# A four-layer attention kernel on Trainium2: the output projection of an item in halves between the next item's scores, and a plainer end of the quantised layer's stages

## The chip, the cores and the metric

The kernel runs on one core of one Trainium2 chip. The metric is the device time of one execution in microseconds (us). Before the change three runs gave 2229.62, 2235.7 and 2238.51 us; the median is 2235.7 us. All times in this text are measured on the chip; "at 1092.91" means so many us after the start of the profiled execution.

The core has five engines that run side by side, each through its own list of instructions in a fixed order: TensorE (PE, matrix products into the accumulator memory PSUM), VectorE (DVE), ScalarE (ACT), GpSimd (POOL), and SyncE (SP), which here issues transfers (DMA). An instruction waits on semaphores for the results that it needs, and everything behind it in its engine's list waits with it.

## The reference

Four layers work on x of 8 items x 256 tokens x 320 channels, with a context of 120 tokens x 192 channels for each item.

- L0: self attention, cross attention over the context, and a gated feed-forward part, each added to x. Its attention is quantised in the reference's way: q, k and v are each divided by (largest absolute value of the whole tensor / 127), rounded to whole numbers and multiplied back; the softmax weights are rounded likewise, in steps of (largest weight / 255). There are 20 heads of 16 channels.
- L1: self attention, cross attention and a gated feed-forward part, not quantised.
- L2: attention over the first 104 context tokens and, with a softmax of its own, over the last 16; both are summed and projected. In the profile this is "both".
- L3: attention with 8 heads over the context and over a few further tokens whose queries are made through x itself. In the profile this is "last".

In short, for one attention with residual:

```python
q, k, v = fq_sym(x @ Wq), fq_sym(ctx @ Wk), fq_sym(ctx @ Wv)      # fq_sym only in L0
w = softmax(einsum('bhnd,bhmd->bhnm', q, k) * dh ** -0.5)
w = fq_zero(w)                                                    # only in L0
x = x + einsum('bhnm,bhmd->bhnd', w, v).reshape(b, n, c) @ Wo + bo
```

## The kernel before

**Two parts.** `tile_xattn_kernel` (L1622) first runs L0's two attentions through two objects of class `Quant`, `s` for self and `c` for cross. Since a quantisation step needs the largest value of the whole tensor, these go stage by stage over all eight items. All other work is `run_flow` (L667): 40 items (four feed-forward blocks of L0, then eight self, eight cross, four feed-forward, eight "both", eight "last") in a pipeline.

**The order of the work.** The kernel is written as generators. `weave` (L649) and `run_flow` take one step of each live generator in turn, and what a step issues is put at the end of the engines' lists. A scheduler behind it may still move single instructions within an engine. So the order in which generators are taken in a round, and the places of their `yield`s, set which of two pieces of work comes first on each engine.

**`run_flow`.** At step s it runs four generators: `tops` of item s+1 (largest scores), `project` of item s+2 (norm, transposes, q, k, v), `fin` of item s-1 (output projection), and `out` of item s (softmax and values), in this order before the change. Within one item of heads:

- `top_scores` (L398): `max_scores` (L374) makes the scores of a query tile against all keys on PE (L385) into PSUM pairs, and DVE takes the negated largest value of each row (L392, `negm`). PE then transposes `negm` (L409), ScalarE copies it to `nT`, and five transfers on SP put it into rows of `qT` (`qT<-nT`), so that the next pass subtracts the maximum within the product.
- `weighted` (L415): `exps(g)` makes the scores again, transposed (L430), and ScalarE the exponentials (`e`, L436); `values` multiplies them with v and with ones (L447); DVE's reciprocal (L455) and multiply (L456) give `oT`. There are five head groups; `exps(0)` comes before the first `yield`, then one group for each round.
- `project_out_steps` (L472): the residual with bias on POOL (L477); then for each of the two token tiles t a `yield`, the product of `oT` with the output weights (L120: three matmuls of 128x320, five for "both", where `oT` has five parts), and the addition to x on DVE (L483). `out` ends with the first step of it, so `fin` has the two halves left. The reductions, the scores and the transposes work on PSUM tiles in rotation: `pair()` (`pf`) and `bank()` (`pa`).

**The quantised layer.** `project_all` (L1207) makes q, k and v of each self item; ScalarE copies them from PSUM (`Q`, `K`, `V`), and `top` (L1201) takes the largest absolute values on DVE (L1202). The last item's q and k are read in PSUM directly, in four reductions. `steps` (L1319) brings the maxima of all partitions together through two transposes (L489 to L496) and makes the steps (`sc`). `whole` (L1339) turns q and k of an item into whole numbers in bf16, in five passes: `tk` and `tq` (scaled, with a large constant added, L1347 and L1350), the constant subtracted from `tk` twice under two masks of heads (`K`, L1353 and L1357), and from `tq` (`Q`, L1363 or L1362). For item 0 (`fast`) DVE takes `tk` and `K`, POOL `tq`, and ScalarE `Q`; all other items go through `whole_all` (L1390) on POOL, except item 1 of the cross part, which is `fast` too. `tops_all` (L1407) makes the scores (L1422) and their maxima (L1425). `out_all` (L1547) makes weights, values (L1563) and the output projection; alongside it, `queries_all` (L1284) makes the cross part's q: `norm`, `turn` (transposes, L330), three `project`s for each item, at rounds of a table `at`.

Of the kernel before, what the change touches and what calls it, by code (L numbers as in the profile page):

```python
# [18 lines left out]
P = 128  # L19
# [35 lines left out]
class Kernel:  # L55
# [118 lines left out]
    def open_quant(self, pool):  # L174

        nc = self.nc

        self.place = pool.tile([P, G, PAD], F32, name="place")
        nc.gpsimd.memset(self.place, 0.0)
        for g in range(G):  # L180
            nc.gpsimd.memset(self.place[:, g, 15 + g : 30 : G], 1.0)

        self.magic = pool.tile([P, 1], F32, name="magic")
        nc.gpsimd.memset(self.magic, -MAGIC)
        self.fill = pool.tile([P, 1], F32, name="fill")
        self.rows = pool.tile([P, 3], F32, name="rows")
        for i in range(3):
            nc.vector.tensor_reduce(self.rows[:, i : i + 1], self.m32[:, 15 + G * i : 30], AX.X, ALU.add)
        nc.vector.tensor_scalar(self.fill, self.rows[:, 0:1], -1e6, 1e6, ALU.mult, ALU.add)
        nc.vector.tensor_scalar(self.rows[:, 1:], self.rows[:, 1:], -1.0, None, ALU.mult)  # L190
        self.sel = pool.tile([P, 2, G, P], BF16, name="sel")
        col = pool.tile([P, 2, G], F32, name="selc")
        for i in range(2):
            nc.vector.tensor_reduce(
                col[:, i], self.m32[:, : 15 * (i + 1)].rearrange("p (i g) -> p g i", g=G), AX.X, ALU.add
            )
            nc.vector.tensor_copy(self.sel[:, i], col[:, i].unsqueeze(2).to_broadcast([P, G, P]))
        self.npx = pool.tile([P, TPB, 4, PAD], BF16, name="npx")
        nc.gpsimd.memset(self.npx, 0.0)
        self.nTs = pool.tile([P, B, N], BF16, name="nTs")  # L200
        self.sums = pool.tile([P, B, N], F32, name="sums")
# [196 lines left out]
    def top_scores(self, qT, kT, nk, segs):  # L398

        nc = self.nc  # L400
        negm = self.small.tile([P, len(segs), 4, G, TPB], F32, tag="negm", name="negm")
        yield from self.max_scores(qT, kT, nk, segs, negm)
        yield
        nT = self.work.tile([4 * G, len(segs), N], F32, tag="nT", name="nT", bufs=1)
        for n in range(len(segs)):
            ps = self.bank()
            nv = negm[:, n].rearrange("p j g t -> p (j g) t")
            for t in range(TPB):
                nc.tensor.transpose(ps[: 4 * G, t * P : (t + 1) * P], nv[:, :, t], self.ident)  # L409
            nc.scalar.copy(nT[:, n, :], ps[: 4 * G, :N])  # L410
            for g in range(G):
                r = n if g in (1, 3) else D + n
                nc.sync.dma_start(qT[r::PAD, g, :], nT[g::G, n, :])
# [253 lines left out]
    def run_flow(self, items, before={}, after={}):  # L667


        n = len(items)  # L670
        made = {}
        for step in range(-2, n + 1):
            if step + 2 < n:
                if step + 2 in before:
                    before[step + 2]()
                made[step + 2] = items[step + 2]()
            order = ((step + 1, 1), (step + 2, 0), (step - 1, 3), (step, 2))
            gens = [made[i][k]() for i, k in order if 0 <= i < n]
            while gens:
                for g in list(gens):  # L680
                    try:
                        next(g)
                    except StopIteration:
                        gens.remove(g)
            if step in after:
                after[step]()

# [492 lines left out]
class Quant:  # L1180
# [5 lines left out]
    def __init__(self, k, pool, kpool, ln, w, brow, cross):  # L1186
        self.k, self.pool, self.kpool, self.ln, self.w, self.brow, self.cross = k, pool, kpool, ln, w, brow, cross
        self.kc, self.ks = (1, M) if cross else (TPB, P)
        self.nk = self.kc * self.ks

        per = 2 // self.kc
        self.units = [(range(g, min(G, g + per)), h) for g in range(0, G, per) for h in range(2)]
        nc = k.nc
        n = "c" if cross else "s"
        self.am = pool.tile([P, 3, B + 2], F32, name=f"am_{n}")
        nc.gpsimd.memset(self.am, 0.0)
        self.sc = pool.tile([P, 16], F32, name=f"sc_{n}")
        self.q, self.kk, self.v = {}, {}, {}


    def top(self, i, b, src):  # L1201
        self.k.nc.vector.tensor_reduce(  # L1202
            self.am[: src.shape[0], i, b : b + 1], src, AX.XY if len(src.shape) > 2 else AX.X, ALU.max,
            apply_absolute_value=True,
        )

    def project_all(self):  # L1207
# [11 lines left out]
        for b in range(B):  # L1219
# [26 lines left out]
                nc.scalar.copy(dst[:, :2], ps[:, :, :N])  # L1246
                nc.scalar.copy(dst[:, 2], ps[:, i, N:])
            self.top(2, b, v)
            if b + 1 < B:
                self.top(0, b, q)  # L1250
                self.top(1, b, kt)
                continue

            for i, ps in enumerate((pq, pk)):
                self.top(i, b, ps[:, :, :N])
            for i, ps in enumerate((pq, pk)):
                self.top(i, B, ps[:, i, N:])

    def keys_all(self):

# [23 lines left out]
    def queries_all(self):  # L1284
# [4 lines left out]
        def norm(b):  # L1289
            x[b] = k.normed(b, self.ln, on=nc.gpsimd if b + 1 < B else None)  # L1290
# [6 lines left out]
        def project(b, m):  # L1297
            ps = k.pair()
            k.mm(ps[:, 0, :N], [(w["q"][:, c, m * P : (m + 1) * P], xT[b][:, c, :]) for c in range(3)])
            nc.scalar.copy(self.q[b][:, m * N : (m + 1) * N], ps[:, 0, :N])  # L1300
            if b + 1 == B:
                self.top(0, b + m, ps[:, 0, :N])
            elif m == 2:
                self.top(0, b, self.q[b])

        at = {b: [5 * b + i for i in (0, 3, 6, 7, 8)] for b in range(B - 2)}
        at[B - 2] = [5 * B - 10 + i for i in (0, 3, 4, 5, 7)]
        at[B - 1] = [5 * B - 10 + i for i in (3, 6, 7, 8, 9)]  # L1310
        for r in range(5 * B):
            for b in range(B):
                for i, n in enumerate(at[b]):
                    if n == r:
                        norm(b) if i == 0 else turn(b) if i == 1 else project(b, i - 2)
            yield


# [20 lines left out]
    def whole(self, b, fast=False):  # L1339
# [4 lines left out]
        to = nc.vector if fast else nc.gpsimd  # L1344
        q, kt = self.q[b], self.kk[b]
        tk = k.work.tile([P, 3 * N], F32, tag="xT", name="tk")
        to.tensor_scalar(tk[:, : 3 * nk], kt, sc[:, 7:8], MAGIC, ALU.mult, ALU.add)  # L1347
        yield
        tq = k.work.tile([P, 3 * N], F32, tag="xh", name="tq")
        nc.gpsimd.tensor_scalar(tq, q, sc[:, 6:7], MAGIC, ALU.mult, ALU.add)  # L1350
        yield
        kh = self.kk[b] = kt.bitcast(BF16)[:, : 5 * nk].rearrange("p (c n) -> p c n", n=nk)
        to.tensor_scalar(  # L1353
# [5 lines left out]
        )  # L1359
        yield  # L1360
        qh = self.q[b] = q.bitcast(BF16)[:, : 3 * N].rearrange("p (c n) -> p c n", n=N)
        if fast:  # L1362
            nc.scalar.activation(qh.rearrange("p c n -> p (c n)"), tq, AF.Identity, bias=k.magic)  # L1363
        else:
            to.tensor_scalar(qh.rearrange("p c n -> p (c n)"), tq, MAGIC, None, ALU.subtract)

    def whole_v(self, b):

# [21 lines left out]
    def whole_all(self):  # L1390

        for b in range(1, B):
            n = 0
            for _ in self.whole(b, self.cross and b == 1):
                n += 1
                yield
            for _ in range(len(self.units) - n):
                yield
# [115 lines left out]
    def weight_steps(self):  # L1514
# [3 lines left out]
        nc.scalar.activation(k.sums, k.sums, AF.Ln)  # L1518
        part = k.small.tile([P, 2], F32, tag="part", name="part")
        least = k.small.tile([P, 1], F32, tag="least", name="least")  # L1520
        nc.vector.tensor_reduce(least, self.am[:, 0, :B], AX.X, ALU.min)
        nc.vector.reciprocal(part[:, 0:1], least)
        most = k.small.tile([P, 2], F32, tag="most", name="most")
        if self.cross:
            nc.vector.tensor_reduce(part[:, 1:2], self.am[:, 2, :B], AX.X, ALU.max)
            k.all_max(most, part)
            nc.vector.tensor_copy(sc[:, 2:3], most[:, 1:2])
            self.step_of(2, 3)
        else:
            k.all_max(most[:, :1], part[:, :1])  # L1530
# [16 lines left out]
    def out_all(self):  # L1547
# [42 lines left out]
            pass  # L1590
        self.shift(0)
        todo, projects = [], {}
        for r in range(rounds * B + 2):
            b, i = divmod(r, rounds)
            if b < B:
                w = weights(b, groups[i])
                if i == 0:
                    more = self.whole_v(b + 1) if b + 1 < B else iter(())
                todo.append((b, groups[i], w))
            while len(todo) > (2 if b < B else 0):  # L1600
                values(*todo.pop(0))


            for t in range(TPB):
                d, left = divmod(r - 2 - t, rounds)
                if r == rounds * B + 1:
                    d, left = B, 0
                if left == 0 and 1 <= d <= B:
                    if t == 0:
                        projects[d] = project(d - 1)  # L1610
# [11 lines left out]
def kernel(ctx: ExitStack, tc: tile.TileContext, a, out):  # L1622
    k = Kernel(ctx, tc, a, out)
    with ExitStack() as es:
# [15 lines left out]
        with tc.tile_pool(name="l0", bufs=1) as pool:  # L1640
            k.open_quant(pool)
            with tc.tile_pool(name="l0_keys", bufs=1, side="right") as kpool:
# [10 lines left out]
                    c.top(1, b, c.kk[b])  # L1653
                s.weight_steps()
                v = c.values_all()
                k.weave((0, s.out_all()), (8, c.queries_all()), (5 * B + 1, islice(v, 3)))
            fp = ff.enter_context(tc.tile_pool(name="w_ff1", bufs=1, side="right"))
            context = ExitStack()
            k.open_context(context.enter_context(tc.tile_pool(name="context", bufs=1, side="right")), dram)
# [133 lines left out]
```

## Time and profile before

| What | Before |
|---|---|
| median of three runs | 2235.7 us |
| profiled execution | 2235.43 us |
| its span (first to last instruction) | 2233.4 us |
| mean granted TensorE clock, share of full speed | 0.965 |
| L0's two attentions, 0 to about | 672 us |
| self items of L1, a step | 38.1 us |
| cross items of L1, a step | 22.5 us |
| "both" items, a step | 25.3 us |

The profile is one execution on the chip. Its group rows read: line, engine, operation, output<-inputs, shape and type, x count | busy us, mean ns of one | idle us of the engine just before them, and what ended most of it. The tables of waits give: who waits at which line, "<-" the engine and line that released it: us in all, times, longest. The timelines give: start in us, duration in us, engine, line, operation, x count, and in brackets the idle time before. A matmul of 32*128 uses 32 rows of the array, four of them running side by side; one of 128*128 uses it whole.

### The profile page before, as it was taken

The page shows a single profiled execution, that of the slowest core. Times are in us where ns is not written, and L with a number is a line of the kernel's source. Part 1 is how long each engine was busy: PE and PEld are TensorE (multiplying, and loading weights), DVE is VectorE, ACT ScalarE, POOL GpSimd, SP SyncE. Part 2 cuts the span into 40 slices and gives each one's busy share as a digit, 9 for nine tenths or more (in the row PEclk, how much of TensorE's full clock was granted, in tenths as well). Part 3 has the DMA queues.
Part 4 walks back from the last instruction along what each step waited for, and adds up shares of the span by engine and source line. Part 5 has one row for each costly group of instructions (what it writes and reads, how often), then busy time and mean ns, then how long its engine had stood idle before and what let it go on. Part 6 is the DMA issues. An engine that isn't in the chain of part 4 may idle for free.

```text
span 2233.4 us, 38265 instructions
## 1 busy us (share of the span) xinstructions
PE 2044.5 (92%) x16413; PEld 1201.3 (54%) x16413; DVE 1117.4 (50%) x1698; ACT 825.7 (37%) x1252; POOL 357.9 (16%) x365
## 2 busy tenths in 40 slices
PE   6889878898899999999999999899999799999997
PEld 5643345554444555465555555554555455666664
DVE  4388677555752221335655667611121466556465
ACT  2347878467532121124444443411201233222221
POOL 1092066601411000000000001100000100000100
PEclk9989889898889999999999999999999899999999
DMA  4000000642110000020000001100000201000000
GB/s 117 17 12 2 1 1 4 167 111 57 55 53 28 1 0 1 1 92 2 2 2 22 27 25 35 47 1 0 1 1 2 68 25 32 12 24 26 23 19 16
DMA packets 79303, 63.21 MB, mean 28 GB/s; under 512 B 48410, under 2 KB 68318, under 8 KB 78622
## 3 DMA queue, kind: packets, MB, share of 16 engines
q1 hardware_dynamic: 75070, 57.06, 9.3%
q10 hardware_dynamic: 4064, 3.71, 0.6%
q8 instruction: 129, 2.11, 0.4%
q14 instruction: 40, 0.33, 0.1%
HBM read 42.61 MB, written 17.37 MB: 27 GB/s over the span
## 4 chain that ended last, share of the span: by engine, by line
PE 75%; DVE 16%; ACT 5%; issue 3%; DMA 1%; POOL 1%; SPq 0%; ACTq 0%; DVEq 0%; POOLq 0%
PE pf L120 13%; PE pf L584 13%; PE pf L132 9%; PE pa L120 7%; PE pa L447 6%; PE pf L430 4%; PE pa L584 3%; PE pf L139 3%; PE pf L385 3%; DVE negm L1425 3%; PE pf L1466 3%; PE pf L728 3%; DVE rs L455 2%; PE pa L1488 2%; DVE negm L392 2%
## 5 line engine op out<-in xcount | busy, mean ns | idle before, releaser
L436 ACT ACTIVATE e<-pf 128x1024 f32<-128x1024 f32 (+2 forms) x176 | 158.3, 944 | 234.9 <-PE pf L430 227.8
L392 DVE TENSOR_REDUCE negm<-pf 128x4 f32<-128x1024 f32 (+4 forms) x224 | 188.1, 886 | 108.8 <-PE pf L385 108.8
L584 PE MATMUL pf<-xTf,ff 128*128 128x512 f32 x512 | 232.4, 601 | 5.2 <-DVE negm L392 5.2
L455 DVE RECIPROCAL rs<-pa 128x256 f32<-128x256 f32 x88 | 152.2, 1745 | 144.0 <-PE pa L447 144.0
L477 POOL TENSOR_TENSOR xb<-x_sb,brow 128x640 f32<-128x640 f32 x40 | 62.2, 1555 | 792.2 <-DVE x_sb L483 748.2
L1473 ACT ACTIVATE e<-pf,sc_s 128x1024 f32<-128x1024 f32 x160 | 169.6, 1116 | 49.4 <-PE pf L1466 42.6
L1425 DVE TENSOR_REDUCE negm<-pf 128x4 f32<-128x1024 f32 (+2 forms) x128 | 143.3, 1134 | 68.1 <-PE pf L1422 61.4
L611 DVE SCALAR_TENSOR_TENSOR hT<-pf,cols_sb,gl 128x512 f32<-128x512 f32 x64 | 48.0, 751 | 256.8 <-ACT gl L610 254.5
L120 PE MATMUL pf<-ff,hT 128*128 128x320 f32 x640 | 174.4, 434 | 0.0
L584 PEld LDWEIGHTS pf<-xTf,ff 128*128 128x128 f32 x512 | 94.9, 191 | 125.2 <-issue 119.8
L120 PEld LDWEIGHTS pf<-ff,hT 128*128 128x128 f32 x640 | 120.9, 190 | 55.5 <-issue 6.1
L430 PE MATMUL pf<-qT,kT 32*128 32x256 f32 (+1 forms) x1280 | 122.3, 411 | 21.9 <-DMA qT<-nT 12.8
L610 ACT ACTIVATE gl<-pf,cols_sb 128x512 f32<-128x512 f32 x64 | 43.9, 687 | 248.0 <-PE pf L584 248.0
L385 PE MATMUL pf<-kT,qT 32*128 32x120 f32 (+1 forms) x1920 | 114.8, 329 | 18.3 <-ACT e L436 18.1
L120 PE MATMUL pa<-o,oT 128*128 128x320 f32 x352 | 105.4, 441 | 15.2 <-DVE oT L456 14.1
L385 PEld LDWEIGHTS pf<-kT,qT 32*128 32x128 f32 x1920 | 84.9, 189 | 58.4 <-ACT e L436 27.7
L1466 PE MATMUL pf<-Q,K 32*128 32x256 bf16 (+1 forms) x960 | 90.5, 294 | 25.3 <-DVE negm L1425 13.2
L639 POOL TENSOR_TENSOR xb<-x_sb,brow 128x640 f32<-128x640 f32 x16 | 25.1, 1566 | 543.1 <-DVE x_sb L644 528.7
L447 PE MATMUL pa<-e,v 128*32 128x256 f32 (+1 forms) x1280 | 105.2, 388 | 2.3 <-ACT e L436 1.7
L1581 DVE TENSOR_SCALAR w<-e 128x1024 bf16<-128x1024 f32 (+2 forms) x128 | 87.4, 691 | 37.5 <-ACT e L1473 36.3
L430 PEld LDWEIGHTS pf<-qT,kT 32*128 32x128 f32 (+1 forms) x1280 | 68.7, 183 | 68.3 <-issue 37.3
L132 PE MATMUL pf<-xT,q 128*128 128x256 f32 x384 | 101.0, 392 | 0.4 <-ACT e L436 0.2
(287 smaller groups left out, 3448.1 us busy)
## 6 DMA issues: line engine op xcount, KB each, us to landing
ff<-in_L_xattn_Wff_dram SPq DMA_DIRECT2D x1, 2560.0 KB
qT<-nT SPq DMA_DIRECT2D x160, 4.0 KB
ff<-in_L_xattn_ff_w_dram SPq DMA_DIRECT2D x1, 2560.0 KB
out_dram<-x_sb SPq DMA_DIRECT2D x16, 160.0 KB
kd_cross<-kst SPq DMA_DIRECT2D x8, 300.0 KB
vd_cross<-vst SPq DMA_DIRECT2D x8, 300.0 KB
vd_both<-vst SPq DMA_DIRECT2D x8, 300.0 KB
kT<-kd_cross SPq DMA_DIRECT2D x8, 300.0 KB
```

The lines of the kernel that those rows point to most:

```text
L120: self.nc.tensor.matmul(out, l, r, start=i == 0, stop=i == len(pairs) - 1)
L132: self.nc.tensor.matmul(o, *t[c], start=start and c == 0, stop=stop and c == n - 1, skip_group_check=True)
L385: nc.tensor.matmul(s[j // 2][:, j % 2, o : o + nk], qT[r : r + PAD, g, t * P : (t + 1) * P], kT[r : r + PAD, g, :nk], start=True, stop=True,)
L392: nc.vector.tensor_reduce(negm[:, n, 2 * i : 2 * i + 2, g0 : g0 + len(gs), :].rearrange("p j g t -> p j (g t)"), sv[:, :, :, k0:k1], AX.X, ...
L430: nc.tensor.matmul(s[j // 2][:ks, j % 2, o : o + N], kT[r : r + PAD, g, c * ks : (c + 1) * ks], qT[r : r + PAD, g, :], start=True, stop=True,)
L436: nc.scalar.activation(e[:ks, 2 * i : 2 * i + 2, :n], s[i][:ks, :, :n], AF.Exp, scale=scale)
L447: nc.tensor.matmul(o[j * PAD : (j + 1) * PAD, what * N : (what + 1) * N], w, es[g][:ks, j, c * N : (c + 1) * N], start=first and c == 0 an ...
L455: nc.vector.reciprocal(rs, o[:, N:])
L584: ins = nc.tensor.matmul(*args, **kw)
L1425: nc.vector.tensor_reduce(negm[:, 2 * h : 2 * h + 2, gs[0] : gs[-1] + 1, :].rearrange("p j g t -> p j (g t)"), s[:, :, : len(gs) * TPB * n ...
L1466: nc.tensor.matmul(s[at // 2][:ks, at % 2, o : o + N], l, m, start=not shift and o == 0, stop=shift and o + N == n, skip_group_check=True,)
L1473: nc.scalar.activation(e[:ks, :, :n], ps[:ks, :, :n], AF.Exp, scale=self.sc[:ks, 9:10])
```

## The change

It has six parts.

1. In `run_flow` the first round of a step goes `tops`, `project`, `out`, `fin`, and all later ones `tops`, `project`, `fin`, `out`. So `exps(0)` of an item is issued ahead of the first half of the previous item's output projection, and the second half follows a round later, ahead of the item's first values.
2. `top_scores` keeps its extra `yield` only where there are fewer keys than N = 256. In self items the transposes of `negm`, the copy `nT` and the five transfers are issued one round earlier.
3. `project_all` takes the last item's largest |q| and |k| from the copies, as for all items. `queries_all` does so for its last item, and its table of rounds becomes the same for all items (44 rounds in place of 40). `am` loses two columns.
4. `whole`: `tk` is always made on POOL; `tq` and the last pass `Q` on DVE for a `fast` item. ScalarE's pass and its constant (`magic`) go.
5. `whole_all`: item 1 of the cross part is no longer `fast`; all its passes go to POOL.
6. `out_all` has two more rounds, issues at most one group of values in a round also at its end, and takes the last item's two projection halves in rounds of their own. `values_all` starts three rounds later.

```diff
@@ top_scores
         yield from self.max_scores(qT, kT, nk, segs, negm)
-        yield
+        if nk < N:
+            yield
@@ run_flow
-            order = ((step + 1, 1), (step + 2, 0), (step - 1, 3), (step, 2))
-            gens = [made[i][k]() for i, k in order if 0 <= i < n]
+            tops, project, out, fin = (
+                made[i][k]() if 0 <= i < n else iter(()) for i, k in ((step + 1, 1), (step + 2, 0), (step, 2), (step - 1, 3))
+            )
+
+            gens = [tops, project, out, fin]
             while gens:
...
+                gens = [g for k in (tops, project, fin, out) for g in gens if g is k]
@@ project_all
-            if b + 1 < B:
-                self.top(0, b, q)
-                self.top(1, b, kt)
-                continue
-
-            for i, ps in enumerate((pq, pk)):
-                self.top(i, b, ps[:, :, :N])
-            for i, ps in enumerate((pq, pk)):
-                self.top(i, B, ps[:, i, N:])
+            self.top(0, b, q)
+            self.top(1, b, kt)
@@ queries_all
-            if b + 1 == B:
-                self.top(0, b + m, ps[:, 0, :N])
-            elif m == 2:
+            if m == 2:
                 self.top(0, b, self.q[b])
-        at = {b: [5 * b + i for i in (0, 3, 6, 7, 8)] for b in range(B - 2)}
-        at[B - 2] = [5 * B - 10 + i for i in (0, 3, 4, 5, 7)]
-        at[B - 1] = [5 * B - 10 + i for i in (3, 6, 7, 8, 9)]
-        for r in range(5 * B):
+        todo = {0: norm, 3: turn, 6: lambda b: project(b, 0), 7: lambda b: project(b, 1), 8: lambda b: project(b, 2)}
+        for r in range(5 * B + 4):
             for b in range(B):
-                for i, n in enumerate(at[b]):
-                    if n == r:
-                        norm(b) if i == 0 else turn(b) if i == 1 else project(b, i - 2)
+                if r - 5 * b in todo:
+                    todo[r - 5 * b](b)
@@ whole
-        to.tensor_scalar(tk[:, : 3 * nk], kt, sc[:, 7:8], MAGIC, ALU.mult, ALU.add)
+        nc.gpsimd.tensor_scalar(tk[:, : 3 * nk], kt, sc[:, 7:8], MAGIC, ALU.mult, ALU.add)
...
-        nc.gpsimd.tensor_scalar(tq, q, sc[:, 6:7], MAGIC, ALU.mult, ALU.add)
+        to.tensor_scalar(tq, q, sc[:, 6:7], MAGIC, ALU.mult, ALU.add)
...
-        if fast:
-            nc.scalar.activation(qh.rearrange("p c n -> p (c n)"), tq, AF.Identity, bias=k.magic)
-        else:
-            to.tensor_scalar(qh.rearrange("p c n -> p (c n)"), tq, MAGIC, None, ALU.subtract)
+        to.tensor_scalar(qh.rearrange("p c n -> p (c n)"), tq, MAGIC, None, ALU.subtract)
@@ whole_all
-            for _ in self.whole(b, self.cross and b == 1):
+            for _ in self.whole(b):
@@ out_all
-        for r in range(rounds * B + 2):
+        for r in range(rounds * B + 4):
...
-            while len(todo) > (2 if b < B else 0):
+            if len(todo) > (2 if b < B else 0):
                 values(*todo.pop(0))
...
-                if r == rounds * B + 1:
-                    d, left = B, 0
@@ tile_xattn_kernel
-                k.weave((0, s.out_all()), (8, c.queries_all()), (5 * B + 1, islice(v, 3)))
+                k.weave((0, s.out_all()), (8, c.queries_all()), (5 * B + 4, islice(v, 3)))
```

More of the change, by code (lines that the diff above doesn't have):

```diff
@@ L181, in open_quant @@
             nc.gpsimd.memset(self.place[:, g, 15 + g : 30 : G], 1.0)
-        self.magic = pool.tile([P, 1], F32, name="magic")
-        nc.gpsimd.memset(self.magic, -MAGIC)
         self.fill = pool.tile([P, 1], F32, name="fill")
@@ L1194, in __init__ @@
         n = "c" if cross else "s"
-        self.am = pool.tile([P, 3, B + 2], F32, name=f"am_{n}")
+        self.am = pool.tile([P, 3, B], F32, name=f"am_{n}")
         nc.gpsimd.memset(self.am, 0.0)
@@ L1202, in top @@
         self.k.nc.vector.tensor_reduce(
-            self.am[: src.shape[0], i, b : b + 1], src, AX.XY if len(src.shape) > 2 else AX.X, ALU.max,
-            apply_absolute_value=True,
+            self.am[: src.shape[0], i, b : b + 1], src, AX.XY if i == 2 else AX.X, ALU.max, apply_absolute_value=True
         )
@@ L1520, in weight_steps @@
         least = k.small.tile([P, 1], F32, tag="least", name="least")
-        nc.vector.tensor_reduce(least, self.am[:, 0, :B], AX.X, ALU.min)
+        nc.vector.tensor_reduce(least, self.am[:, 0, :], AX.X, ALU.min)
         nc.vector.reciprocal(part[:, 0:1], least)
@@ L1524, in weight_steps @@
         if self.cross:
-            nc.vector.tensor_reduce(part[:, 1:2], self.am[:, 2, :B], AX.X, ALU.max)
+            nc.vector.tensor_reduce(part[:, 1:2], self.am[:, 2, :], AX.X, ALU.max)
             k.all_max(most, part)
```

## The prediction

> **What bounds the kernel now.** First the engine table, the chain that ended last and two groups of the page:
>
> ```profile
> PE 2044.5 (92%) x16413; PEld 1201.3 (54%) x16413; DVE 1117.4 (50%) x1698; ACT 825.7 (37%) x1252; POOL 357.9 (16%) x365
> ...
> PE 75%; DVE 16%; ACT 5%; issue 3%; DMA 1%; POOL 1%; SPq 0%; ACTq 0%; DVEq 0%; POOLq 0%
> ...
> L430 PE MATMUL pf<-qT,kT 32*128 32x256 f32 (+1 forms) x1280 | 122.3, 411 | 21.9 <-DMA qT<-nT 12.8
> ...
> L120 PE MATMUL pa<-o,oT 128*128 128x320 f32 x352 | 105.4, 441 | 15.2 <-DVE oT L456 14.1
> ```
>
> TensorE (PE) is the bound, and it executes in the order written. So the change can only add or remove PE's idle time. The waits of PE, summed (us in total, times, longest), show what is there to win:
>
> ```profile
> PE pf L385 <- ACT e L436: 18.1, 22, 1.0
> PE pa L120 <- DVE oT L456: 14.1, 13, 1.9
> ...
> PE pf L430 <- DMA qT<-nT: 12.8, 1, 12.8
> PE pf L430 <- DVE negm L392: 7.5, 12, 1.9
> ```
>
> The moved projection (L120) waits 14.1 us for oT; the L385 behind it 18.1 us for an exponential. The one DMA wait of 12.8 is at the first "both" step, where the order of instructions is unchanged. Now PE's timeline in one self step (start, us, idle before it in brackets), then VectorE's (DVE's):
>
> ```profile
> 1092.91 1.15 PE L385 MATMUL pf<-kT,qT 32*128 32x256 f32 x16
> 1093.98 0.88 PE L330 MATMUL pf<-ident,xh 128*128 128x128 f32 x6
> 1094.70 1.78 PE L120 MATMUL pa<-o,oT 128*128 128x320 f32 x6
> 1096.41 1.76 PE L430 MATMUL pf<-qT,kT 32*128 32x256 f32 x14
> ...
> 1099.17 1.13 PE L385 MATMUL pf<-kT,qT 32*128 32x256 f32 x12 [0.77 <-ACT e L436]
> 1100.23 1.08 PE L120 MATMUL pa<-o,oT 128*128 128x320 f32 x3
> ```
>
> ```profile
> 1092.72 1.76 DVE L455 RECIPROCAL rs<-pa 128x256 f32<-128x256 f32 x1 [2.74 <-PE pa L447]
> ...
> 1094.85 2.35 DVE L392 TENSOR_REDUCE negm<-pf 128x4 f32<-128x1024 f32 x2
> ```
>
> Here the projection does not wait. Its three matmuls of token tile 0 fill the time in which DVE finishes reciprocal, multiply (0.42) and two reductions; the scores at 1096.41 need the PSUM that those reductions read.
>
> **Self steps (six of them, where the three L120 go behind the eight L430).** Two things move. The transposes of the maxima (L409, 0.33 of PE, then a ScalarE copy and five SP transfers) come one round earlier, ahead of the last values matmuls: these and DVE's chain behind them start 0.33 later, so the reductions end near 1097.5, not 1097.20. The earlier transfers win nothing, as no self step waits for one; on SP they pass only other transfers without a waiter. And L430, without L120 ahead of it, is reached at 1094.8, waits for the first reduction until 1096.45 and for the second until 1097.58. Queued behind it on PE are L120, L385 and the second L120; for them wait ScalarE's next exponentials and DVE's residual add (L483), statistics and norm. After it: 0.97 for the rest of L430, 1.81 for L120 (1.45, and 0.36 for its last matmul and the changes of tile), 1.08 for L385 (its wait of 0.77 is gone, as the exponential is long done): 1097.58 + 0.97 + 1.81 + 1.08 = 1101.44, against 1100.23. That is +1.2 a step, +7.2 for six. From below, +0.9: DVE's chain is not late after all, and the 0.33 falls out. From above, +1.5: L120's second half also meets DVE late. I take 1.2 because every term of it but the 0.33 is a duration of the rows. At the passage to the cross steps the nT copy stands before an exponential on ScalarE (0.3) and DVE's chain is late: +0.5.
>
> **Cross steps (six).** One matmul of the projection stays ahead of L430, two move:
>
> ```profile
> 1318.23 1.85 PE L120 MATMUL pa<-o,oT 128*128 128x320 f32 x6 [1.10 <-DVE oT L456]
> ```
> ```profile
> 1318.33 2.21 DVE L392 TENSOR_REDUCE negm<-pf 128x8 f32<-128x960 f32 x2
> ```
>
> The one that stays takes over the wait of 1.10, so that isn't won. Then L430 would start near 1318.6 but waits for the two reductions, at 1319.45 and 1320.54; the two moved matmuls come after it. The exponential's wait of 0.79 goes, the reductions' comes: by the same sum the second token tile is at 1324.0, not 1323.59, +0.4, and tile changes make it +0.5: +3.0 (0 to +4.5).
>
> **"Both" steps (five).** Three of five matmuls stay ahead, two move:
>
> ```profile
> 1818.51 2.93 PE L120 MATMUL pa<-o,oT 128*128 128x320 f32 x10 [1.11 <-DVE oT L456]
> 1821.37 1.14 PE L430 MATMUL pf<-qT,kT 32*120 32x256 f32 x16
> ...
> 1823.68 1.15 PE L385 MATMUL pf<-kT,qT 32*128 32x120 f32 x28 [0.97 <-ACT e L436]
> ```
>
> The 1.11 stays. L430 then needs nothing late (three matmuls cover the reductions), its exponential starts 1.08 earlier and the wait of 0.97 goes. Less tile changes: −0.85 each, −4.2 (0 to −5).
>
> [...] L120 uses the whole array (128*128), L430 and L385 a quarter of its rows (32*128); L120 between them makes two more changes in each of 17 steps. From the starts in the trace: L120 to L120 269 ns, L120 to L430 362; the way out costs some 50. That is 0.14 a step, 2.4 in all. The sums above hold it; by idle time alone they would be 2.4 lower.
>
> **The quantised layer.** Its whole-number passes stand on the path before the first scores of the self part (PE idle 3.06) and of the cross part (3.03):
>
> ```profile
> 107.94 0.62 DVE L1347 TENSOR_SCALAR tk<-K,sc_s 128x768 f32<-128x768 f32 x1
> ...
> 108.59 1.15 DVE L1353 TENSOR_SCALAR K<-tk,half 128x768 bf16<-128x768 f32 x1
> ...
> 109.78 1.00 DVE L1357 TENSOR_SCALAR K<-tk,half 128x512 bf16<-128x512 f32 x1
> ```
> ```profile
> 108.09 1.24 POOL L1350 TENSOR_SCALAR tq<-Q,sc_s 128x768 f32<-128x768 f32 x1 [3.31 <-DVE sc_s L1329]
> ```
>
> After the change POOL makes tk, and DVE tq, the Q pass (ScalarE's 0.93 before), and both K passes. [...] By the uncontended 0.62 the chain of DVE is 0.62 + 0.16 + 0.62 + 0.2 + 0.62 + 0.5 from 107.94: done at 110.7, about as now. [...] K's 1.15 ends 0.41 after POOL's end at 109.33. So I place one DVE pass after each POOL pass: Q ends 109.74, K 110.92 (after POOL's next, at 110.5), K's second 112.05 (after POOL's 0.9 more); it ended at 110.78 before. The first reductions follow it: +1.2 (0 to 1.5).
>
> The cross part in the same way, POOL's passes being 0.56 (tk), 0.90 (tq) and 1.49 (K) long: DVE's tq ends 412.67, POOL's tk 413.10 and item 1's tk 413.66, K 413.9, POOL's tq 414.65, K's second 414.8, POOL's K of item 1 416.2, DVE's Q 416.7. First scores 416.75, not 414.45: +2.3 (if Q slips in ahead of that K, +0.8). Item 1, now wholly on POOL (some 6 us), is ready near 420, and its scores begin near 433: nothing; without that cover it would cost up to 6.
>
> Edits at about nothing: the last item's |q| and |k| from copies, 2 x 0.95 in place of 692 + 692 + 415 + 415 ns, −0.3 less a later start: 0 (±0.5). The last query's maximum, 0.95 on a copy in place of 0.42: half a us later, under PE's key projection, which runs until 410.30: 0 (+2 without it). Its later rounds: norm, turn and projection take 4.8 us under 6.9 of PE work: 0. out_all's tail: PE waits 0.94 for oT at 668.3, half goes: −0.5. The remaining flow steps: 0 ±0.5.
>
> **Sum.** 7.2 + 0.5 + 3.0 − 4.2 + 1.2 + 2.3 − 0.5 = +9.5. The profiled execution took 2235.43 (span 2233.4), so 2244.9; it lies 0.3 under the median of the runs, 2235.7, so 2245.2. A measurement of this kernel tells 0.5% (11.2 us) from no change: the bounds are 2224.5 and 2246.9, and the forecast is just inside.
>
> **Rivals.**
> *Slower:* in the self steps the exponential's wait (longest 1.0) stays behind the new wait for reductions. For it: L385 writes the PSUM that ScalarE reads, and the exponential starts only when L430 has run. Against it: L120's 1.81 now lies between. Price 1.0 x 6 = +6, so 2251; it passes the bound from 0.3 a step.
> *The order only shifts idle time:* PE takes up the delay at the step's other waits, and only the quantised layer's +3.0 is left: 2238.7. For it: 92% busy on PE, so idle time exists. Against: I found no further wait inside a self step.
> *Faster:* the projection's waits vanish (14.1), the exponential's with them in eleven steps (11 x 0.85 = 9.4), against +3.0: 2215.2. For it: the two largest waits. Against: oT is still awaited by the matmuls that stay ahead.
>
> **Numbers.** Forecast 0.50 (its own range 2240 to 2251, four tenths of it above 2246.9), slower rival 0.25, shifted idle time 0.18, faster 0.07. Hence faster 0.07, within 0.48, slower 0.45. Leaving out the faster case and the top: 2236 to 2255.
>
> **What would show it.** Right: the waits of L120 for oT fall little (14.1 to 11 or more), L430's for negm rise from 7.5 by 12 or more, L385's for e fall from 18.1 to under 8; a self step is 1.2 longer; the first scores' waits (3.06, 3.03) grow by 1 and 2. Wrong: the L430 waits do not appear, or the self steps, 38.1 us apart in the trace, keep that distance.

## The result, and the profile after

The changed kernel takes 2247.06 us (median of ten runs), the kernel before 2233.4 us (median of ten, the three shown above among them). The ratio is 1.0063, 95% interval 1.0043 to 1.0084: it became slower by 0.6%, some 14 us. The time lies inside the forecast's own range of 2240 to 2251 us; its sum of +9.5 us lies at the lower edge of what was measured (+9.6 to +18.8). That is in part luck: two things that the sum did not hold, one of some +14 us and one of some -7, partly cancel.

The page of the changed kernel, in the rows that answer to those shown of before (lines have moved: L429 is the old L430, L383 the old L385, L390 the old L392):

```profile
PE 2061.9 (92%) x16413; PEld 1208.4 (54%) x16413; DVE 1118.4 (50%) x1693; ACT 822.8 (37%) x1249; POOL 363.6 (16%) x368
...
PE 75%; DVE 16%; ACT 4%; issue 3%; SPq 2%; DMA 1%; POOL 1%; ACTq 0%; DVEq 0%; POOLq 0%
...
L429 PE MATMUL pf<-qT,kT 32*128 32x256 f32 (+1 forms) x1280 | 133.7, 423 | 33.2 <-DVE negm L390 24.5
...
L120 PE MATMUL pa<-o,oT 128*128 128x320 f32 x352 | 120.7, 482 | 13.0 <-DVE oT L455 11.9
```

The same 16413 matmuls keep TensorE busy for 17.4 us more (2061.9 against 2044.5). L120 of the projection alone goes from 105.4 to 120.7 us, with the same 352 matmuls: a mean of 482 ns in place of 441. The prediction took the length of a matmul as given; this is the first sign of what it lacked. The waits of TensorE in the whole execution:

```profile
PE pf L429 <- DVE negm L390: 24.5, 27, 2.4
...
PE pa L120 <- DVE oT L455: 11.9, 11, 1.1
...
PE pf L429 <- DMA qT<-nT: 7.4, 1, 7.4
...
PE pf L383 <- ACT e L435: 2.5, 4, 0.8
```

These moved as forecast: the projection still waits for oT (14.1 to 11.9), the wait of the scores for the reductions goes from 7.5 to 24.5, that of L383 for the exponential from 18.1 to 2.5. One self step of the changed kernel, on TensorE:

```profile
1049.13 1.15 PE L383 MATMUL pf<-kT,qT 32*128 32x256 f32 x16
1050.20 0.88 PE L328 MATMUL pf<-ident,xh 128*128 128x128 f32 x6
1052.67 2.26 PE L429 MATMUL pf<-qT,kT 32*128 32x256 f32 x16 [1.59 <-DVE negm L390]
1054.86 1.88 PE L120 MATMUL pa<-o,oT 128*128 128x320 f32 x6
1056.67 1.15 PE L383 MATMUL pf<-kT,qT 32*128 32x256 f32 x16
1057.75 1.88 PE L120 MATMUL pa<-o,oT 128*128 128x320 f32 x6
```

Where L120 stood there is now a wait of 1.59, and the second token tile starts 8.62 us after L383's first matmul (1057.75 - 1049.13), before 7.32 (1100.23 - 1092.91). VectorE's reciprocal starts 0.14 after that L383 (1049.27), before 0.19 ahead of it (1092.72): its chain is 0.33 later, as forecast. From one step to the next, between the last reciprocals (L455, then L454) of successive items, this is 39.20 us against 38.10. But the next step took 42.48, with the same instructions. Its busy time and granted clock (columns: stretch, its length, PE busy and matmuls, granted clock, DMA share, GB/s):

```profile
1086.23:1089.64 3.41, 3.41 (x54) 1.00 0.01 4
1089.64:1093.06 3.42, 1.82 (x15) 1.00 0.00 0
1093.06:1096.47 3.41, 3.41 (x13) 0.51 0.00 0
1096.47:1099.88 3.41, 3.41 (x16) 0.50 0.02 5
1099.88:1103.30 3.42, 3.42 (x34) 0.99 0.00 0
```

In the stretch with the wait TensorE was busy for 1.82 of 3.42 us, and the two stretches after it ran at half the clock. In this trace the half clock comes in 24 pieces. All but the last, which the end of the execution cuts, are 3.41 us long or a multiple of it (up to 20.48), and all start on one raster of 3.41 us, to within 0.001 us; the 19 pieces of the kernel before do the same. From the first self step to the last cross step these pieces sum to 51 us in the changed kernel; in the kernel before it is one piece of 3.4. The part from the first reciprocal of the self items to the last of the cross items takes 475.4 us (987.70 to 1463.08), before 444.8 (997.39 to 1442.19): 30.6 us more, of which the steps' lengths at full clock explain 11.

In the rest of the execution the changed kernel shows less half clock, not more (the quantised layer 109 against 126 us, both and last items 24 against 30; the feed-forward blocks have one piece of 3.4 more), and it reaches the self items 9.7 us earlier. That cannot be put down to the change: two runs described below (e3 and e8) have the same order of instructions up to there, and reach them at 997.63 and 989.93, with 130 and 109 us of half clock in the quantised layer. So these two profiled executions are only 4.3 us apart, where the medians are 14 apart.

The both steps, and one cross step, of the changed kernel:

```profile
1835.43 1.85 PE L120 MATMUL pa<-o,oT 128*128 128x320 f32 x6 [1.12 <-DVE oT L455]
1837.22 1.14 PE L429 MATMUL pf<-qT,kT 32*120 32x256 f32 x16
1838.29 1.34 PE L120 MATMUL pa<-o,oT 128*128 128x320 f32 x4
1839.56 1.17 PE L383 MATMUL pf<-kT,qT 32*128 32x120 f32 x32
```
```profile
1331.71 0.78 PE L120 MATMUL pa<-o,oT 128*128 128x320 f32 x2 [1.09 <-DVE oT L455]
1333.02 2.19 PE L429 MATMUL pf<-qT,kT 32*120 32x256 f32 x16 [0.52 <-DVE negm L390]
1335.13 1.34 PE L120 MATMUL pa<-o,oT 128*128 128x320 f32 x4
```

Both steps: the wait for oT stays, the exponential's 0.97 is gone; a step is 1.03 shorter (24.28 for 25.31). Cross steps: the wait for oT stays and one for the reductions comes; a step is 0.43 longer (22.95 for 22.52) where the clock is whole, 3.6 longer (26.16) where it isn't.

The whole-number passes of the self part on VectorE, after:

```profile
106.07 1.15 DVE L1350 TENSOR_SCALAR Q<-tq 128x768 bf16<-128x768 f32 x1
...
107.26 1.14 DVE L1341 TENSOR_SCALAR K<-tk,half 128x768 bf16<-128x768 f32 x1
108.32 1.12 DVE L1345 TENSOR_SCALAR K<-tk,half 128x512 bf16<-128x512 f32 x1
```

Each of them ends 0.3 to 0.4 us after a POOL pass (POOL's tk, item 1's tk and its tq end at 106.81, 107.99 and 109.17), as the prediction placed them, and takes over 1.1 us. In the cross part the last one did not:

```profile
413.60 0.54 DVE L1350 TENSOR_SCALAR Q<-tq 128x768 bf16<-128x768 f32 x1
```

The last stage, which the prediction put at nothing, is the other surprise. From the last reciprocal of the both items to the end it takes 271.3 us, before 278.9. The step before that is 0.62 shorter too; 1.1 of the whole lies in the last 37 us, where the half clock fell differently, so that some 7 us are won at full clock. Here is TensorE in one step of it, before and then after (L1065 is L1068 in the changed kernel):

```profile
2028.18 0.60 PE L1065 MATMUL pf<-cs,kz 32*128 32x192 f32 x6
2028.71 1.88 PE L120 MATMUL pa<-lwo,oT 128*128 128x320 f32 x6
2030.52 0.61 PE L1065 MATMUL pf<-cs,kz 32*128 32x192 f32 x8
2031.06 0.81 PE L120 MATMUL pa<-lwo,oT 128*128 128x320 f32 x2
...
2031.80 0.42 PE L1065 MATMUL pf<-cs,kz 32*128 32x192 f32 x1
...
2032.07 0.32 PE L1065 MATMUL pf<-cs,kz 32*128 32x192 f32 x1
```
```profile
2037.71 0.93 PE L1068 MATMUL pf<-cs,kz 32*128 32x192 f32 x16
2038.58 2.42 PE L120 MATMUL pa<-lwo,oT 128*128 128x320 f32 x8
```

Before, the projection cut the sixteen score matmuls into pieces of 6, 8, 1 and 1: 0.60 + 0.61 + 0.42 + 0.32 us (some of these rows overlap others), with two more changes between matmuls of 32 and of 128 rows. After, sixteen together take 0.93; they start in fours, each four within 0.02 us.

### The profile page after: what moved, and what is told of

It is laid out like the page before. It is cut to its first block, busy times and chain, and to the rows that moved or that the text cites. A ratio compares the mean times of both kernels' runs of the same rounds, so it can differ in the third digit from the quotient of the medians.

```text
span 2237.9 us, 38256 instructions
## 1 busy us (share of the span) xinstructions
PE 2061.9 (92%) x16413; PEld 1208.4 (54%) x16413; DVE 1118.4 (50%) x1693; ACT 822.8 (37%) x1249; POOL 363.6 (16%) x368
## 4 chain that ended last, share of the span: by engine, by line
PE 75%; DVE 16%; ACT 4%; issue 3%; SPq 2%; DMA 1%; POOL 1%; ACTq 0%; DVEq 0%; POOLq 0%
PE pf L583 13%; PE pf L120 12%; PE pf L132 9%; PE pa L120 7%; PE pa L446 6%; PE pf L429 5%; PE pa L583 3%; PE pf L139 3%; PE pf L383 3%; DVE negm L1410 3%; PE pf L731 3%; PE pf L1451 3%; DVE rs L454 2%; PE pa L1473 2%; DVE negm L390 2%
## 5 line engine op out<-in xcount | busy, mean ns | idle before, releaser
L390 DVE TENSOR_REDUCE negm<-pf 128x4 f32<-128x1024 f32 (+4 forms) x224 | 187.9, 885 | 81.8 <-PE pf L383 81.7
L454 DVE RECIPROCAL rs<-pa 128x256 f32<-128x256 f32 x88 | 152.3, 1745 | 145.7 <-PE pa L446 145.7
L120 PE MATMUL pf<-ff,hT 128*128 128x320 f32 x640 | 174.4, 434 | 0.0
L429 PE MATMUL pf<-qT,kT 32*128 32x256 f32 (+1 forms) x1280 | 133.7, 423 | 33.2 <-DVE negm L390 24.5
L120 PEld LDWEIGHTS pf<-ff,hT 128*128 128x128 f32 x640 | 120.9, 190 | 55.5 <-issue 6.1
L120 PE MATMUL pa<-o,oT 128*128 128x320 f32 x352 | 120.7, 482 | 13.0 <-DVE oT L455 11.9
L429 PEld LDWEIGHTS pf<-qT,kT 32*128 32x128 f32 (+1 forms) x1280 | 75.9, 188 | 80.8 <-DVE negm L390 45.8
L383 PE MATMUL pf<-kT,qT 32*128 32x120 f32 (+1 forms) x1920 | 111.2, 341 | 2.8 <-ACT e L435 2.5
L383 PEld LDWEIGHTS pf<-kT,qT 32*128 32x128 f32 x1920 | 81.4, 199 | 49.4 <-issue 33.0
L1566 DVE TENSOR_SCALAR w<-e 128x1024 bf16<-128x1024 f32 (+2 forms) x128 | 87.5, 692 | 37.4 <-ACT e L1458 36.3
```

What stands on the lines that cost most here:

```text
L120: self.nc.tensor.matmul(out, l, r, start=i == 0, stop=i == len(pairs) - 1)
L383: nc.tensor.matmul(s[j // 2][:, j % 2, o : o + nk], qT[r : r + PAD, g, t * P : (t + 1) * P], kT[r : r + PAD, g, :nk], start=True, stop=True,)
L390: nc.vector.tensor_reduce(negm[:, n, 2 * i : 2 * i + 2, g0 : g0 + len(gs), :].rearrange("p j g t -> p j (g t)"), sv[:, :, :, k0:k1], AX.X, ...
L429: nc.tensor.matmul(s[j // 2][:ks, j % 2, o : o + N], kT[r : r + PAD, g, c * ks : (c + 1) * ks], qT[r : r + PAD, g, :], start=True, stop=True,)
L454: nc.vector.reciprocal(rs, o[:, N:])
```

## The experiments

Three theories stood after this. *Idle time:* the change costs what its waits cost at full clock; summed over the traces' full-clock steps that is +11 in self and cross steps, -5 in both steps, -7 in the last stage, +1.5 in the quantised layer's two starts, so about 0, which is not what was measured. *Idle time and clock:* the waits of the self and cross steps also bring half-clock pieces. *The quantised layer:* it carries the loss.

**The two parts of the change apart.** First the quantised layer's edits without the flow's, then the flow's two edits without the layer's:

```diff
# e1: Quant, open_quant and the weave's offset as after; run_flow and top_scores as before
# e2: the other way round
```

> The kernel before with the quantised layer's edits alone (maxima from copies, whole-number passes, rounds of queries and out_all); the flow as before. Theory of idle time: the two starts of scores lose 0.7 and 0.8 us as in the profile after, out_all's end wins up to 0.5: +1 us, ratio 1.0005, 0.999 to 1.002. Rival (the quantised layer carries most of the loss of 14 us): +8 or more, ratio 1.0035 or more.

> The kernel before with the flow's two edits alone (the order of fin and out, the yield of top_scores). Theory of idle time alone: six self steps at +1.1, six cross steps at +0.43, five both steps at -1.03 and 0.5 at the passage make +4.5 us, ratio 1.002. Theory of idle time and clock: the waits of 1.6 us in the self and cross steps also bring windows of half clock, which cost some 3.2 us each; with three to eight of them more than before +10 to +20 us, ratio 1.0045 to 1.009, and the trace has several half-clock windows between the first self and the last cross step, where the kernel before has at most one.

Measured: 1.0007 (0.9995 to 1.0020) for the layer, 1.0062 (1.0042 to 1.0082) for the flow. So the flow carries the loss, as large as the whole change's 1.0063, and the layer is at most 0.2%: the third theory falls. The theory of idle time alone, with 1.002, lies outside the flow's interval, and its +4.5 did not yet hold the gain of the last stage, which makes the distance larger. In the flow's trace the half clock sums to 58 us between the first self and the last cross step, in the layer's to 3.4. The granted clock over this part of the execution, for the kernel before, the changed one and the flow alone:

```profile
980.00:1445.00 465.00, 434.76 (x4815) 1.00 0.08 23
```
```profile
980.00:1445.00 465.00, 435.43 (x4560) 0.95 0.06 16
```
```profile
980.00:1445.00 465.00, 435.78 (x4522) 0.94 0.06 16
```

In the same 465 us TensorE is busy as long (434.8, 435.4, 435.8) and finishes 4815, 4560 and 4522 matmuls.

**The flow's two edits apart.**

```diff
# e3: run_flow as after, top_scores with its yield as before
# e4: top_scores without the yield, run_flow as before
-        yield
+        if nk < N:
+            yield
```

> The flow's order of fin and out alone, the yield as before. Theory of idle time: the 0.33 us by which the transposes delay VectorE falls out of six self steps, so +4.5 - 2 = +2.5 us, ratio 1.001. With the clock: the wait in a self step shrinks from 1.6 to about 1.3 us, and the windows of half clock in self steps become fewer or vanish, those of the cross steps stay: +4 to +10 us, ratio 1.002 to 1.0045.

> The missing yield of top_scores alone (self items' transposes, copy and transfers one round earlier). Theory: the projection still covers VectorE's chain, so a self step gains or loses at most 0.3 us: ratio 0.999 to 1.001, no half-clock windows in the self steps. Rival (the earlier transposes are themselves a cause): +2 us or more, ratio over 1.001, with new waits of the scores for the reductions.

Measured: 1.0072 (1.0048 to 1.0095) for the order, 0.9992 (0.9975 to 1.0009) for the yield. The yield does nothing without the new order: a self step is 38.23 us, not 38.10, since L120 covers VectorE's chain. With the new order it adds little: the full-clock self step is 39.07 without the change of the yield (seen in e8, below) and 39.20 with it. My expectation for the order alone was too low. The wait of 1.27 us that remains still has half a clock behind it: in that trace a piece of 3.41 us follows in each of five self steps, which take 40.72 instead of 39.07, and 44 us of half clock come together.

**Filling the wait.** If the clock is what costs, then TensorE kept busy with nothing useful in the wait should win time back. In the steps concerned the transposes of the norm's output are issued three times over, into the same place:

```diff
-        for i, n in CH:
-            for t in range(TPB):
+        for _ in range(times):          # 3 for self items from b = 3 on and cross items but b = 1
+            for i, n in CH:
+                for t in range(TPB):
...
```

> The flow's two edits alone, and the transposes of the norm's output (twelve more, the same ones again, 1.3 us of TensorE) repeated in those self and cross steps that wait for the reductions, just ahead of the wait; they compute nothing new. Theory of clock: TensorE is no longer idle there, the half-clock windows of the self and cross steps vanish (under 14 us of them, where the flow alone had 58), the steps keep their full-clock lengths of 39.2 and 18.2 us, and the kernel loses the clock's part: ratio 0.997 to 1.000, though it does more work. Theory without the clock (the steps are long because of waits alone): the work that is added costs time or nothing, ratio 1.006 or more.

Measured: 1.0036 (1.0022 to 1.0050), against the flow's 1.0062 (1.0042 to 1.0082). TensorE does more work, and the kernel is faster by about 0.26%, some 6 us. The two kernels were timed on different chips, each against its own runs of the kernel before, and the intervals overlap a little. The traces are clearer: from the first reciprocal of the self items to the last of the cross items the flow alone takes 478.4 us and the filled kernel 463.0. A self step of it:

```profile
1096.75 2.18 PE L331 MATMUL pf<-ident,xh 128*128 128x128 f32 x18
1099.21 0.70 PE L433 MATMUL pf<-qT,kT 32*128 32x256 f32 x4 [0.28 <-DVE negm L394]
1100.34 1.13 PE L433 MATMUL pf<-qT,kT 32*128 32x256 f32 x12 [0.43 <-DVE negm L394]
```
```profile
980.00:1445.00 465.00, 440.28 (x4814) 0.99 0.08 21
```

The idle 1.59 is down to 0.28 and 0.43, each of five successive self steps takes 39.20, and none has a half-clock piece; 13.7 us of half clock are left, at the passages and in cross steps. So the self steps' length of 39.20 is the wait's, and what lay above it was the clock's. My number (0.997 to 1.000) was too good: in a cross step the twelve matmuls do not fit into the wait (23.49 where 22.95 was the full-clock length, six times 0.54), and the pieces at the passages stay. The theory without the clock (1.006 or more) is excluded by the interval.

**The stages apart.** The order of before is kept in one part of the flow and changed in the other; the yield stays as before in both:

```diff
+            late = step >= 25        # e5: both and last items in the new order;  e8: step < 25, the others
+            gens = [tops, project, out, fin] if late else [tops, project, fin, out]
```

> The kernel before, with the new order of fin and out only from the first both step on (both and last items), the old order in the self and cross steps. Theory of idle time and clock: five both steps win 1.03 each and the last stage 9 us, as in the traces of the changed kernels, and no half-clock windows come in the self and cross steps: -14 us, ratio 0.9935, 0.991 to 0.996. Rival (the last stage's 9 us come from elsewhere, or are chance): -5 us, ratio 0.998.

> The new order only up to the cross items and the second feed-forward part; the both and last items as before. Theory of idle time and clock: 6 self steps at +0.9 and six cross steps at +0.43, 0.5 to 2.6 at the passages, and some 45 us of half clock at about half their length: +25 to +30 us, ratio 1.011 to 1.013. Rival (sizes of the stages' parts wrong): the same as the order in all steps, 1.007.

Measured: 0.9945 (0.9919 to 0.9971) with the new order only at the end, 2218.0 us in the median, which is faster than both kernels; and 1.0102 (1.0078 to 1.0126) with the new order only before it, a little under my number. Both rivals (0.998 and 1.007) lie outside the intervals. The clock of the self and cross steps, in the first and then in the second:

```profile
980.00:1445.00 465.00, 434.85 (x4830) 1.00 0.08 22
```
```profile
980.00:1445.00 465.00, 437.74 (x4628) 0.96 0.06 17
```

In the first trace the self and cross steps have their old lengths (38.10, 22.52), the both steps the new one (24.28), and the last stage takes 269.9 us, in place of 278.9; in the second it is 278.6. The last stage's gain is therefore the order's, and not chance. Five of its items took 36.3, 34.9, 34.9, 35.2 and 36.3 us and now take 34.4 each, all at full clock. TensorE's idle time in the five falls only from 8.2 to 6.9 us, its busy time from 169.5 to 165.0: most of the gain is the uncut score matmuls. The two items that lost most by the cuts (1.9 against 0.6) had them in pieces of 4, 4, 6, 1 and 1, and a wait of 0.55 us behind them for an exponential (`ef`).

**The sum, run by run.** The clock records of the two traces, before and after, hold only full and half clock (1.0 and 0.5). If that is so in every run, the mean granted clock of each run gives its time at half clock. Taking 0.47 us of loss for each us of it (from the self steps, see below) gives this estimate, in us against the kernel before. The steps at full clock are the parts read from the traces: self steps +7.7 with the changed yield and +6.5 without it, cross steps +3.7, both steps -5.2, the last stage -7.1, the fill +3.2.

| Run | steps at full clock | more half clock, mean of the runs | estimate in all | measured, 95% |
|---|---|---|---|---|
| e2, flow | -0.9 | 36.0 | +16 | +13.8 (9.4 to 18.3) |
| e3, order | -2.1 | 40.1 | +17 | +16.1 (10.7 to 21.2) |
| e5, late | -12.3 | 2.3 | -11 | -12.3 (-18.1 to -6.5) |
| e6, filled | +2.3 | 12.7 | +8 | +8.0 (4.9 to 11.1) |
| e8, early | +10.2 | 33.1 | +26 | +22.7 (17.4 to 28.1) |

All five fall within their intervals; the steps at full clock alone do so only for e5. Since the columns come from the same traces and runs, this shows that the account adds up; it is no forecast. The runs of one kernel show the same: the flow's fourteen go from 2229.09 us at a mean clock of 0.966 to 2255.62 at 0.954, and those two that kept 0.963 or more (2229.09 and 2232.94) lie about the median of the kernel before, 2231.59.

## Why the prediction was right, and where it was not

*Self steps* (+7.2, and +0.5 at the passage): right in mechanism and, at full clock, in size. Five steps lost 1.10 each, the sixth 1.55 (36.07 in the filled kernel, 34.52 before) and the following one 0.67: 7.7. Of the 1.10 the change of the yield makes 0.13 (39.20 against 39.07), for which the sum had 0.33.

*Cross steps* (+3.0): right. Six times 0.43 is 2.6, and 1.1 came at the passage to the feed-forward blocks (in the trace of e3, with one piece of half clock in it).

*Both steps* (-4.2): right in mechanism; five times 1.03 is -5.2, a little beyond the range given (0 to -5). The deduction for changes of tile (0.14 a step) was too large here.

*The remaining flow steps at 0 ±0.5:* wrong. The last stage is among them, and the sum put it at nothing without giving a reason. What its rows held was mostly a cost of cutting, busy time: sixteen matmuls in pieces of 6, 8, 1 and 1 have rows of 1.95 us in sum, in one piece of 0.93, and the item shown became 0.56 shorter (34.93 to 34.37), 0.08 of it idle time. With the waits that went too the stage made some -7, the largest gain of the change. The changes between matmuls of 128 and of 32 rows, which I counted against the change (starts 362 ns apart in place of 269 on the way in; the 50 ns of the way out were my estimate), spoke for it in this stage: two changes fewer for each item shown.

*The quantised layer's starts* (+1.2 and +2.3): the order that I had placed, one DVE pass behind each POOL pass, was right in the self part (ends 0.41, 0.41 and 0.28 us after POOL's). From the copy that brings the maxima (sc, L496) to the first scores it took 3.65 us in place of 3.02, to the first reductions 4.56 in place of 3.67, so +0.6 to +0.9 in place of +1.2. In the cross part I chose the wrong one of two orders: the Q pass, from 413.60, took 0.54, and POOL's K pass, from 413.53, lasted 1.88 and not 1.49. The start cost +0.8, the lower end that I had named. The waits before the first scores grew from 3.06 to 3.69 and from 3.03 to 3.85, not by 1 and 2. The whole layer came to 1.0007.

*What no step held: the clock.* The sum took every duration from rows at full clock, and treated a wait as worth its own length. In the self steps of e3 and of the changed kernel a wait of 1.27 to 1.6 us in one piece of 3.41 us was followed by 3.4 or 6.8 us at half clock, which made a self step longer by 1.65 or 2.9 to 3.3 on top. In the traces of the order's kernels these pieces sum to 41 to 58 us, where the kernel before has 3.4; at about 0.47 us of loss for each us of it (3.1 of 6.8, 1.65 of 3.4) that is an estimate of 18 to 26 us in those executions. The full-clock sum of all parts is near 0 and the measured difference +14: about 14 us remain for the clock in the runs of the changed kernel, somewhat less than its trace suggests (for the kernel before, the clock of most of the runs that go with it is not on record). Whether a piece followed a given wait went, in the self steps, with how the wait fell into the raster of 3.41 us on which the pieces start: in the trace of the changed kernel all four waits of 1.59 us that lie in one piece of the raster were followed by half clock, and the two that are split over two pieces (1.07 and 0.52, 1.31 and 0.29) were not. It did not always go so: in the flow's trace one that is split into 0.88 and 0.72 was. The runs of one kernel spread with the clock: over ten runs the changed kernel goes from 2237.79 us at a mean clock of 0.959 to 2259.08 at 0.951.

The slower rival (+6 in the self steps) named the right place with the wrong mechanism: the exponential's wait did not stay (18.1 to 2.5). The rival of shifted idle time falls with the self steps' 1.10, the faster one with the 11.9 us of waits for oT that remain.

## What to carry to other kernels

A wait on TensorE need not be worth only its own length (here, of two steps with the same wait of 1.59 us, the one with half clock behind it took 42.48 and the other 39.20): look at how much of a few microseconds around it is idle, and whether the clock row drops behind it. Work that was placed in such a gap may be holding the clock up as well as filling time (the filled kernel had 13.7 us of half clock where the flow alone had 58). Moving it away paid here where something else covered the gap, as in the both steps (24.28 for 25.31). And when a matmul of another tile shape is moved, look at what it cuts in two: the gain may be in busy time (here 0.93 us of rows for 1.95), which no table of waits shows.

## What the runs showed that I had not expected

How short an idle time was enough. Count TensorE's idle time in each piece of the raster of 3.41 us, in the self and cross steps. In the trace of the changed kernel a half-clock piece came behind pieces with 1.31, 1.34, three times 1.59, 1.60, 1.62 and 2.03 us of idle time, and once behind two neighbours with 0.92 and 0.95. In the same trace other pieces with 1.31, 1.35 and 1.59 kept the full clock, and so did all with up to 1.10 but that pair. In the kernel before one piece with 1.88 was followed by half clock; those with up to 1.23 kept the clock, among them three in a row with 0.67, 1.23 and 0.97. So no length of idle time divides the two. What else enters, for instance how many rows of the array the matmuls in that stretch use, was not tried.

And twelve further matmuls in each of twelve steps, computing nothing new, made a kernel faster: 1.0062 to 1.0036.
